# The feed-forward residual over pairs of blocks: output by features, weight leaves stationary, 256 tokens moving

## The chip, the cores and the metric

The kernel runs on one core of a Trainium2 chip. The metric is the device time of one execution in microseconds, the median of three runs. A core has TensorE (PE; its weight loads are listed apart as PEld), VectorE (DVE), ScalarE (ACT), GpSimd (POOL) and SyncE (SP); transfers are issued here from SP and ACT and run on 16 DMA engines. Matmuls write the eight PSUM banks, which GpSimd does not read in this program.

## The reference

A transformer block with conditioning, x of 2 x 2048 tokens by 512 features, all in float32:

```python
emb = jnp.dot(jax.nn.silu(t), ada_w) + ada_b
shift_msa, scale_msa, gate_msa, shift_mlp, scale_mlp, gate_mlp = jnp.split(emb, 6, axis=-1)
norm = _ln(x) * (1.0 + scale_msa[:, None]) + shift_msa[:, None]
h = jax.nn.gelu(jnp.dot(norm, ssm_w1) + ssm_b1, approximate=False)
x = x + gate_msa[:, None] * (jnp.dot(h, ssm_w2) + ssm_b2)
norm2 = _ln(x) * (1.0 + scale_mlp[:, None]) + shift_mlp[:, None]
hf = jax.nn.gelu(jnp.dot(norm2, ff_w1) + ff_b1, approximate=True)
x = x + gate_mlp[:, None] * (jnp.dot(hf, ff_w2) + ff_b2)
```

ff_w1 is 512 x 1024, ff_w2 1024 x 512. Gates, shifts and scales differ between the two batch elements, not between tokens.

## The kernel before

The 4096 tokens are eight blocks of 512 (four tiles of 128). The first part of the program (ssm1, ssm2, norm2) makes x1 = x + gated ssm output for every block and leaves x1 and the normed, turned tokens in DRAM. The second part, the ff part, takes the blocks in four pairs s = 0 to 3: ff1(s) for both blocks at once, then ff2(s, 0) and ff2(s, 1) one block after the other.

All large products use Strassen's scheme in Winograd's form: two halves by two halves give seven products P1 to P7 of half size in place of eight, at the price of sums of the operands (`first` and `second`, four additions each) and of the results. Nested twice, 49 products of quarter size ("leaves") stand for 64.

- ff1 (lines 1025 to 1098): a stage holds seven outer products in the order OUTER, each of seven leaves. The weight leaf is stationary (128 x 128, read from DRAM through a ring of five slots in `ring`), and 256 columns of tokens move: two matmuls a leaf, 98 a stage. Leaves are spread over slots: product n has its leaves at slots 7n, 7n+2, ..., so two products alternate on TensorE. Each leaf is added from its bank into the hidden tile hC by VectorE (or copied by ScalarE), features on partitions, tokens in columns; ScalarE then takes GELU in place.
- ff2 (lines 1115 to 1285): here hidden leaves are stationary and the weights move, 128 columns at a time, so the result comes out by tokens: 49 leaves of two matmuls, 98 a block, 196 a pair (in the first pair P6 is not nested: 8 matmuls of 256 columns replace 14). The results are added from the banks straight onto x1 in the tile rows, and rows is stored, four stores a block. The gate of the ff branch cannot be applied by row, so it is multiplied into ff_w2 beforehand, once per batch element: weight_fw2 for the first, weight_fw2_ahead and weight_fw2_loaded (through DRAM) for the second; the gated bias gb5 is put into the banks before the products begin.

The order on each engine is not written by hand. Every operation is recorded with its reads, writes and costs; `Plan.order` gives each TensorE operation a due time by the sum of the TensorE costs before it, hands these back to all that it depends on, and a list scheduler (`Plan.simulate`) then picks for VectorE, ScalarE, GpSimd and SP the operation that is due first. Additions marked "vg" may go to VectorE or GpSimd; additions that read a bank only to VectorE. Two additions whose operands all lie in SBUF are never placed at the same time on both, by the planner's `lock`. The order so found is the order in the program: an instruction that waits holds all that stand behind it on its engine, transfers on SP and ACT too.

At the end of the program the last block's ff2 stores its quarters as they are finished: the last four VectorE additions each add a leaf's bank onto rows, and stores of 128 KB follow on SP and ACT.

## Time and profile before

| | us |
|---|---|
| median of three runs | 565.51 (565.48 to 566.46) |
| span of the profiled execution, first to last instruction | 563.6 |
| TensorE busy in it | 557.3 |
| VectorE busy | 484.2 |
| GpSimd busy | 377.5 |
| ScalarE busy | 265.3 |
| ff part on TensorE, first matmul to last | 213.46 to 559.97 |

The profiled execution has no time of its own beside its span; the median of the runs stands 1.9 us above that span. In the tables of windows each row is a stretch of the span: its length, then for each engine the busy time and the number of records, then the granted TensorE clock (1.00 is full), the share of the 16 DMA engines' time and what they moved. A float32 matmul is two records, and a busy time of TensorE is not a measure of peak. In a row of groups stand line, engine, operation, output and inputs, shape, count, busy time, mean ns of one, then the engine's idle time before these and what ended it. The line numbers are those of helpers (L294 mm, L304 turn_by_pe, L256 tt, L274 act, L283 copy, L316 dma, L592 turn).

### The profile page before, as it was taken

The numbers are of one execution on the slowest core, as the hardware profiler recorded it, in microseconds if no ns is written. First come the engines' busy times: TensorE is split into PE (matmuls) and PEld (weight loads), VectorE is DVE, ScalarE is ACT, GpSimd is POOL, SyncE is SP. The second block draws the span as 40 slices with busy tenths as digits, with TensorE's granted clock in tenths as the row PEclk, the third lists the DMA queues.
The fourth block names the chain that finished last, engine by engine and source line by source line (L and its number), as shares of the span: only waits on it lengthen the run. The fifth ranks groups of instructions, "written<-read, shape, count | busy, mean of one in ns | idle before, by whom it ended". The sixth has DMA issues, their size and how long they took to land.

```text
span 563.6 us, 10326 instructions
## 1 busy us (share of the span) xinstructions
PE 557.3 (99%) x3553; PEld 506.3 (90%) x3553; DVE 484.2 (86%) x916; ACT 265.3 (47%) x535; POOL 377.5 (67%) x516
## 2 busy tenths in 40 slices
PE   8999999999999999999999999999999999999997
PEld 4888889888898988889998889999889999889997
DVE  5696978888879989898999888989999898789886
ACT  3473866674878845558102346322366222336020
POOL 2887638979826687996656886776785673446670
PEclk9999999999999999999999999999999999999999
DMA  8953799979699788896047989068956041720022
GB/s 315 398 223 84 236 348 317 304 239 323 221 276 368 246 283 267 274 310 203 4 150 246 302 292 318 35 199 283 324 171 203 2 151 44 273 95 30 1 76 74
DMA packets 53057, 119.85 MB, mean 213 GB/s; under 512 B 5473, under 2 KB 10509, under 8 KB 51470
## 3 DMA queue, kind: packets, MB, share of 16 engines
q1 hardware_dynamic: 51842, 118.66, 63.7%
q10 hardware_dynamic: 1164, 0.55, 0.4%
q8 instruction: 28, 0.46, 0.3%
q14 instruction: 23, 0.19, 0.1%
HBM read 77.63 MB, written 40.51 MB: 210 GB/s over the span
## 4 chain that ended last, share of the span: by engine, by line
PE 97%; DMA 1%; DVE 1%; SPq 0%; issue 0%
PE bank L294 96%; DMA fw<-in_L_cond_ada_w_dram 1%; PE bank L304 0%; DVE rows L256 0%; DVE marks L523 0%; SPq L316 0%; DVE ring L256 0%; DVE far L592 0%; DVE turned L657 0%; DVE marks L524 0%; DVE bank L482 0%; DVE mod L485 0%
## 5 line engine op out<-in xcount | busy, mean ns | idle before, releaser
L294 PE MATMUL bank<-turned,ring 128*128 128x256 f32 x896 | 208.6, 380 | 0.2 <-DVE turned L657 0.2
L294 PEld LDWEIGHTS bank<-turned,ring 128*128 128x128 f32 x896 | 167.8, 190 | 22.7 <-DVE turned L657 0.4
L256 DVE TENSOR_TENSOR hidden<-bank,hidden 128x512 f32<-128x512 f32 (+1 forms) x171 | 124.1, 755 | 27.3 <-PE bank L294 25.1
L294 PE MATMUL bank<-near,hidden 128*128 128x256 f32 (+1 forms) x470 | 95.3, 350 | 0.3 <-DVE rows L256 0.2
L294 PEld LDWEIGHTS bank<-near,hidden 128*128 128x128 f32 x470 | 82.1, 190 | 10.0 <-DVE rows L256 0.6
L294 PE MATMUL bank<-fw,hidden 128*128 128x128 f32 x640 | 90.4, 275 | 0.0
L256 DVE TENSOR_TENSOR rows<-bank,rows 128x128 f32<-128x128 f32 (+3 forms) x154 | 79.0, 555 | 10.1 <-PE bank L294 9.3
L294 PE MATMUL bank<-ring 128*128 128x256 f32 x336 | 82.4, 381 | 0.0
L294 PEld LDWEIGHTS bank<-fw,hidden 128*128 128x128 f32 x640 | 81.2, 192 | 0.5
L283 ACT COPY bank<-bank 128x512 f32<-128x512 f32 (+2 forms) x89 | 37.4, 421 | 78.8 <-PE bank L294 77.8
L294 PEld LDWEIGHTS bank<-ring 128*128 128x128 f32 x336 | 63.2, 190 | 10.4 <-ACT bank L283 0.7
L256 POOL TENSOR_TENSOR turned<-turned 128x512 f32<-128x512 f32 (+1 forms) x55 | 61.2, 1125 | 15.1 <-ACT turned L274 9.2
L256 POOL TENSOR_TENSOR hidden<-hidden 128x512 f32<-128x512 f32 (+2 forms) x56 | 49.0, 883 | 29.3 <-DVE hidden L256 11.9
L294 PE MATMUL bank<-fw,far 128*128 128x128 f32 (+2 forms) x644 | 67.6, 278 | 0.5 <-DMA fw<-in_L_cond_ada_w_dram 0.5
L274 ACT ACTIVATE hidden<-hidden,cols 128x512 f32<-128x512 f32 (+1 forms) x66 | 45.3, 713 | 38.4 <-DVE hidden L256 38.2
L294 PEld LDWEIGHTS bank<-fw,far 128*128 128x128 f32 (+1 forms) x644 | 60.9, 167 | 2.5 <-issue 1.5
L294 PE MATMUL bank<-fw,near 128*128 128x128 f32 (+1 forms) x452 | 61.2, 279 | 0.0
L294 PEld LDWEIGHTS bank<-fw,near 128*128 128x128 f32 x452 | 56.0, 192 | 0.4
L256 POOL TENSOR_TENSOR fw<-fw 128x256 f32<-128x256 f32 (+1 forms) x51 | 44.7, 885 | 13.4 <-DVE fw L256 7.2
L274 ACT ACTIVATE turned<-turned,mod,mod 128x512 f32<-128x512 f32 x56 | 41.6, 805 | 9.5 <-DMA turned<-turned 8.5
L256 POOL TENSOR_TENSOR ring<-turned,ring 128x256 f32<-128x256 f32 x37 | 27.3, 747 | 13.6 <-PE bank L294 7.4
L274 ACT ACTIVATE hidden<-bank,cols 128x256 f32<-128x256 f32 x62 | 26.6, 472 | 17.1 <-PE bank L294 16.9
(136 smaller groups left out, 698.7 us busy)
## 6 DMA issues: line engine op xcount, KB each, us to landing
ring<-fw_parts SPq DMA_DIRECT2D x28, 512.0 KB
turned<-far SPq DMA_DIRECT2D x52, 256.0 KB
ring<-fw_parts SPq DMA_DIRECT2D x28, 384.0 KB
rows<-x SPq DMA_DIRECT2D x32, 256.0 KB
turned<-turned SPq DMA_DIRECT2D x32, 256.0 KB
out_dram<-rows SPq DMA_DIRECT2D x28, 256.0 KB
fw_parts<-fw SPq DMA_DIRECT2D x21, 256.0 KB
fw<-in_L_cond_ada_w_dram SPq DMA_DIRECT2D x5, 1024.0 KB
```

The costliest lines, as they stand in the source:

```text
L256: lambda E: E.tensor_tensor(o, a, b, f),
L274: lambda E: E.activation(o, a, func, bias=bias, scale=scale),
L283: plan.add("a", lambda E: E.copy(o, a), [o], [a], {"a": cost}, {"a": cost + 60})
L294: lambda E: E.matmul(o, lhsT, rhs, start=start, stop=stop, skip_group_check=True, **kw),
```

## The change

ff2 is rebuilt in the shape of ff1. It takes a pair of blocks at once (`down`): seven outer products in the order DOWN, each of seven leaves; the leaf of ff_w2 is stationary, 256 columns of the hidden tile move, two matmuls a leaf, 98 a pair. The result comes out by features (features on partitions, tokens in columns) and is summed in `summed`, which has four quarters: blk 0 or 1, lower or upper features. ff1 and ff2 of all pairs form one stream of 56 products (`ff`), each beginning seven slots after the one before; the last product of all starts six slots later still, and so runs alone. ff_w2 is no longer gated: its leaves are made once and kept. ScalarE multiplies the finished quarter by the gate and adds the gated bias, both per partition now. VectorE then turns the quarter back in 32 x 32 squares, four transfers write it to DRAM in bands, one reads it back by tokens, and two additions put x1 (read again, half the features at a time) on it before the store (`quarter_out`). In the last pair three quarters go this way, with stores in halves on SP and ACT; the quarter of the last product is turned back in pieces by TensorE instead (`last_out`), and products P7 and P4 are scaled by the gate as they are added (`scaled_add`).

On TensorE, at the seam of ff1 and ff2 of the first pair, these were the rows (bank numbers; turned and ring are ff1's operands, fw_71 holds the leaves of ff_w2, hidden, near and far the hidden tile and its sums):

```order
L294 MATMUL bank_76<-turned,ring 128x256 x2
L294 MATMUL bank_77<-ring 128x256 x2
L294 MATMUL bank_74<-fw_71,hidden 128x128 x2
L294 MATMUL bank_74<-fw_71,near 128x128 x2
L294 MATMUL bank_73<-fw_71,near 128x128 x4
L294 MATMUL bank_77<-fw_71,hidden 128x128 x2
L294 MATMUL bank_77<-fw_71,near 128x128 x2
```

and these are they now:

```order
L296 MATMUL bank_75<-turned,ring 128x256 x2
L296 MATMUL bank_73<-hidden,fw_71 128x256 x2
L296 MATMUL bank_77<-turned,ring 128x256 x2
L296 MATMUL bank_79<-far,fw_71 128x256 x2
L296 MATMUL bank_76<-turned,ring 128x256 x2
L296 MATMUL bank_73<-far,fw_71 128x256 x2
L296 MATMUL bank_77<-ring 128x256 x2
L296 MATMUL bank_78<-hidden,fw_71 128x256 x2
```

The first ff2 product now alternates with the last of ff1, and each of its instructions moves 256 columns.

On VectorE, the end of the program was this (each row adds a leaf's bank onto rows; two more, of bank_72 and bank_74 as in the middle here, follow):

```order
L256 TENSOR_TENSOR rows<-bank_78,rows 128x2x256
L256 TENSOR_TENSOR rows<-bank_78,rows 128x2x2x256
L256 TENSOR_TENSOR rows<-bank_72,rows 128x2x128
L256 TENSOR_TENSOR rows<-bank_74,rows 128x128
L256 TENSOR_TENSOR rows<-bank_76,rows 128x2x128
L256 TENSOR_TENSOR rows<-bank_76,rows 128x128
```

From the last but one addition of P7 in the last pair on it is now this (rows is `summed`; far in the additions is the x1 tile of the first quarter, in the transposes the tile of the bands; the transposes are those of the quarter r2, blk 1, upper features):

```order
L1049 SCALAR_TENSOR_TENSOR rows<-bank_77,mod_125,rows 128x2x256
L258 TENSOR_TENSOR far<-rows,far 128x512 x2
L1073 STREAM_TRANSPOSE far<-rows 128x4x4x32 x2
L1049 SCALAR_TENSOR_TENSOR rows<-bank_73,mod_125,rows 128x256
L1049 SCALAR_TENSOR_TENSOR rows<-bank_78,mod_125,rows 128x256
L1049 SCALAR_TENSOR_TENSOR rows<-bank_79,mod_125,rows 128x256
```

The additions of the first quarter stand ahead of the last two transposes, and those ahead of all scaled additions of the last product. The last rows of VectorE are these (near takes, in pieces, the quarter that TensorE turned back; the last two rows add x1 to the last two quarters that went through DRAM):

```order
L1049 SCALAR_TENSOR_TENSOR rows<-bank_73,mod_125,rows 128x256
L258 TENSOR_TENSOR near<-bank_72,near 128x2x128
L258 TENSOR_TENSOR near<-bank_74,near 128x2x128
L258 TENSOR_TENSOR near<-rows,near 128x512 x2
L258 TENSOR_TENSOR far<-rows,far 128x512 x2
```

Both quarters that went through DRAM are completed behind all that the last product brings.

On SP, the end was eight stores:

```order
L316 DMA ring<-fw_parts 128x1024
L316 DMA ring<-fw_parts 128x768 x2
L316 DMA out_dram<-rows 128x512 x4
L316 DMA out_dram<-rows 128x2x128 x4
L1501 UNCONDITIONAL_BRANCH
```

and is now this (back_ tensors are the quarters in DRAM, x_7 is x1 of the last block):

```order
L318 DMA back_0_1_116<-far 32x4x256 x2
L318 DMA out_dram<-far 128x2x256
L318 DMA back_1_1_118<-far 32x4x256 x2
L318 DMA rows<-back_0_1_116 128x1024
L318 DMA far<-x_7_87 128x4x256
L318 DMA rows<-back_1_1_118 128x1024
L318 DMA out_dram<-near 128x2x256
L318 DMA out_dram<-near 128x2x128 x2
L318 DMA out_dram<-far 128x2x256
```

The read of quarter back_0_1 stands behind the write of quarter back_1_1, and the read of that one behind a read of x1 into the tile that the first quarter's store has to leave.

The core of the diff:

```diff
@@ -97,6 +98,7 @@
                 due[op.n] = t
                 t += op.cost["p"]
+        due.update((n, t + 6000.0) for n in self.closing)
...
-    def fw2_sixth(plain, leaves):
-        leaves["P6"] = leaves_of(plain, 6)
...
-    def weight_fw2(b, bank):
-        plan.stage = f"weight_fw2 {b}"
...
-        for k in range(KH):
-            tt("v" if bank else "vg", fw2_t[:, k, :], fw2_t[:, k, :], g, ALU.mult)
-        return fw2_operands()
...
-    def weight_fw2_ahead(b):
...
-    def weight_fw2_loaded(b):
...
+    def weight_fw2():
+        plan.stage = "weight_fw2"
+        for k in range(0, KH, 2):
+            dma(fw2_t[:, k : k + 2], fw2[k * P : (k + 2) * P, :].rearrange("(k p) d -> p k d", p=P), lead=100000.0)
+        halves = [(n, slice(n * KH // 2, (n + 1) * KH // 2), slice(n * D // 2, (n + 1) * D // 2)) for n in range(2)]
+        outer = first({f"{e + 1}{o + 1}": fw2_t[:, k, d] for e, _, d in halves for o, k, _ in halves}, thirds(fw2_s), cuts=2)
+        leaves = {}
+        for n, p in enumerate(DOWN):
+            q = {f"{e + 1}{k + 1}": outer[p][:, 2 * k : 2 * k + 2, e * P : (e + 1) * P] for e in range(2) for k in range(2)}
+            leaves[p] = first(q, thirds(fw2_l[:, n]))
+        return leaves
...
+    DOWN = ("P1", "P2", "P3", "P6", "P5", "P7", "P4")
...
+    def chain_banks(n):
+        b = {"y": banks[Y_AT[n % 4]], "x": banks[X_AT[n % 2]], "v": banks[V_AT[n % 2]]}
+        return b
+
+    QUAD = {"P2": "11", "P5": "22", "P6": "12", "P7": "22", "P3": "12", "P4": "21"}
...
+    def scaled_add(o, t, scale):
+        cost = cols(o) / 0.96 + 70
+        plan.add(
+            "v",
+            lambda E: E.scalar_tensor_tensor(o, t, scale, o, ALU.mult, ALU.add),
+            [o],
+            [t, o, scale],
+            {"v": cost},
+            {"v": cost + 85},
+        )
+
+    def columns(s, d, e, blk):
+        k, b = 2 * d + e, (2 * s + blk) // PER_B
+        return gb5[:, k, b : b + 1], mods[5][:, k, b : b + 1]
+
+    def rest_in(s, d, blk, x):
+        half = slice(d * D // 2, (d + 1) * D // 2)
+        dma(x, x1_d[2 * s + blk][:, :, half])
+        return x, out_blk[2 * s + blk][:, :, half]
+
+    def quarter_out(s, d, blk, r, scaled=False):
+        done = summed[:, r]
+        n = quarters[0] % 2
+        for e in range(0 if scaled else 2):
+            act(done[:, e], done[:, e], AF.Identity, *columns(s, d, e, blk))
+        band = cut(bands[n], "p (a c e r) -> p e c a r", a=M, c=C, e=2)
+        for e in range(2):
+            o, a = band[:, e], cut(done[:, e], "p (c a q) -> p c a q", c=C, a=M)
+            plan.add("v", lambda E, o=o, a=a: E.transpose(o, a), [o], [a], {"v": 636}, {"v": 705})
+        closing = s + 1 == NBLK // 2
+        queue = lambda f: "sa"[f % 2] if closing else "s"
+        far_t = back_d[s][d][blk]
+        for f in range(M):
+            dma(far_t[:, f].rearrange("(a q) r -> q a r", a=M), cut(bands[n][f * G : (f + 1) * G], "p (a r) -> p a r", a=M), queue(f))
+        flat = done.rearrange("p e t -> p (e t)")
+        dma(flat, far_t.rearrange("p f r -> p (f r)"))
+        x, to = rest_in(s, d, blk, rest[n])
+        for h in range(2):
+            c = slice(2 * h, 2 * h + 2)
+            o = cut(x[:, c], "p c (e f r) -> p (c e) f r", e=2, f=M)
+            a = cut(flat, "p (f c e r) -> p c e f r", f=M, c=C, e=2)[:, c].rearrange("p c e f r -> p (c e) f r")
+            tt("v" if closing else "vg", o, a, o, ALU.add)
+            if closing:
+                dma(to[:, c], x[:, c], queue(h))
+                plan.closing.append(plan.ops[-1].n)
+        if not closing:
+            dma(to, x)
+        quarters[0] += 1
...
+    def down(s):
+        q = {f"{o + 1}{blk + 1}": hC[:, blk, :, 2 * o : 2 * o + 2, :] for o in range(2) for blk in range(2)}
+        ops = {"P1": q["11"], "P2": q["21"], "P3": q["22"]}
+        inner = {}
+        last = s + 1 == NBLK // 2
+
+        def sums():
+            plan.stage = f"ff2 {s}"
+            a, b, c = whole_s
+            parts("vg", a, q["12"], q["11"], ALU.subtract, 2)
+            parts("vg", b, q["22"], a, ALU.subtract, 2)
+            parts("vg", q["12"], q["22"], q["12"], ALU.subtract, 2)
+            ops.update(P4=c, P5=a, P6=b, P7=q["12"])
+
+        def last_sum():
+            plan.stage = f"ff2 {s}"
+            parts("vg", ops["P4"], q["21"], ops["P6"], ALU.subtract, 2)
+
+        def prepare(n):
+            w = ops[DOWN[n]]
+            v = {f"{k + 1}{h + 1}": w[:, k, :, h * HT : (h + 1) * HT] for k in range(2) for h in range(2)}
+            inner[n] = second(v, thirds(half_s[n % 2]), room=rooms[n % 3] if n < 4 else None)
+
+        def leaf(n, f):
+            p = DOWN[n]
+            bank = chain_banks(14 * s + 7 + n)
+            t = bank[BANK[f]][:, :HT]
+            for k in range(2):
+                mm(t, fw2_leaves[p][f][:, k, :], inner[n][f][:, k, :], f in ("P1", "P5") and k == 0, f in ("P2", "P3", "P4") and k == 1)
+            if f == "P1":
+                copy(bank["x"][:, :HT], t)
+                return
+            quad = QUAD[f]
+            e, h = int(quad[0]) - 1, int(quad[1]) - 1
+            new = f not in ("P7", "P3")
+            part = summed[:, :, e, h * HT : (h + 1) * HT]
+            r0, r1, r2, r3 = [part[:, r] for r in range(4)]
+
+            def add(o, a):
+                tt("v", o, t, a, ALU.add)
+
+            if p in ("P1", "P3"):
+                o = r1 if p == "P1" else r3
+                if new:
+                    copy(o, t)
+                else:
+                    add(o, o)
+            elif p == "P2":
+                add(r0, r1 if new else r0)
+                if f == "P4":
+                    quarter_out(s, 0, 0, 0)
+            elif p == "P6":
+                add(r1, r1)
+            elif p == "P5":
+                add(r2, r1 if new else r2)
+                if f in ("P2", "P7", "P3", "P4"):
+                    tt("vg", r3, r3, r2, ALU.add)
+                    if last:
+                        act(part[:, 1:3], part[:, 1:3], AF.Identity, *columns(s, 1, e, 0))
+                if f == "P4":
+                    quarter_out(s, 0, 1, 3)
+            elif p == "P7":
+                both, wide = part[:, 1:3], t.unsqueeze(1).to_broadcast([P, 2, HT])
+                if last:
+                    scaled_add(both, wide, columns(s, 1, e, 0)[1])
+                else:
+                    tt("v", both, wide, both, ALU.add)
+                if f == "P4":
+                    quarter_out(s, 1, 1, 2, last)
+            elif not last:
+                add(r1, r1)
+                if f == "P4":
+                    quarter_out(s, 1, 0, 1)
+            else:
+                scaled_add(r1, t, columns(s, 1, e, 0)[1])
+                last_out(s, f, quad)
+
+        return sums, last_sum, prepare, leaf
...
+    def last_out(s, f, quad):
+        if not tail:
+            tail["x"], tail["out"] = rest_in(s, 1, 0, cut(kb(near_r, 0, 4), "p (c d) -> p c d", c=C))
+
+        def turned_back(quad):
+            e, h = int(quad[0]) - 1, int(quad[1]) - 1
+            bank = cut(banks[(2, 0)[h]], "p (c e d) -> p c e d", c=2, e=2)
+            for c in range(2):
+                col = slice((2 * h + c) * P, (2 * h + c + 1) * P)
+                turn_by_pe(bank[:, c, e], summed[:, 1, e, col], ident, c == 0 and h not in tail, c == 1)
+            tail[h] = True
+            c, d = slice(2 * h, 2 * h + 2), slice(e * P, (e + 1) * P)
+            x = tail["x"][:, c, d]
+            tt("v", x, bank[:, :, e], x, ALU.add)
+            dma(tail["out"][:, c, d], x, "sa"[e])
+
+        tail.setdefault("due", [])
+        for q in tail["due"]:
+            turned_back(q)
+        tail["due"] = []
+        if f in ("P7", "P2", "P3", "P4"):
+            tail["due"].append(quad)
+        if f == "P4":
+            turned_back(quad)
...
-    def ff2(s, blk, six, wops):
...
+                work.append((f"ff1 {s}", lambda n=n, got=got: got["up"][0](n), lambda f, n=n, got=got: got["up"][1](n, f)))
+            sums, last_sum, prepare, leaf = down(s)
+            at_slot(7 * (first_at + 7) + 7, sums)
+            at_slot(7 * (first_at + 7 + 4) + 3, last_sum)
+            for n in range(7):
+                work.append((f"ff2 {s}", lambda n=n, fn=prepare: fn(n), lambda f, n=n, fn=leaf: fn(n, f)))
+        total = len(work)
+        starts = [7 * n for n in range(total)]
+        starts[-1] += 6
+        for at in range(starts[-1] + 13):
+            for fn in hooks.get(at, ()):
+                fn()
...
-    for s in range(NBLK // 2):
-        if s == 1:
-            fw2_sixth(*ff)
-        if 2 * s == PER_B:
-            ff = weight_fw2_loaded(1)
-            fw2_sixth(*ff)
-        if 2 * s + 2 == PER_B:
-            weight_fw2_ahead(1)
-        ff1(s)
-        if 2 * s + 2 < NBLK and 2 * s + 2 not in SOON:
-            normed2(2 * s + 2)
-        for blk in range(2):
-            ff2(s, blk, *ff)
```

352 lines of the change are left out of this document (74 added, 278 removed).

## Prediction

> **What bounds the kernel now.** I read the page's engine table, then the chain of waits, then a table of windows cut at the stages of the ff part (the ff stages are seen in the timeline of TensorE by their operands: turned and ring for ff1, fw and hidden, near or far for ff2).
>
> ```profile
> PE 557.3 (99%) x3553; PEld 506.3 (90%) x3553; DVE 484.2 (86%) x916; ACT 265.3 (47%) x535; POOL 377.5 (67%) x516
> PE 97%; DMA 1%; DVE 1%; SPq 0%; issue 0%
> 208.18 351.36 PE bank L294 x2348
> 559.56 0.42 DVE rows L256
> 560.01 0.29 DVE rows L256
> ```
>
> TensorE is busy 99% and carries 97% of the chain; from 208.18 to the end it is one piece of 351.36 us that waits for nobody. Only at the end do two VectorE adds follow, and then 563.6 - 560.3 = 3.3 us in which the last stores land. So whatever shortens TensorE's stream shortens the run, as long as the end does not get longer.
>
> ```profile
> core 0: us, PE busy (x) PEld busy (x) DVE busy (x) ACT busy (x) POOL busy (x), PEclk, DMA share, GB/s
> 213.46:255.95 42.49, 42.49 (x197) 37.08 (x196) 38.68 (x63) 23.81 (x39) 39.46 (x53) 1.00 0.92 290
> 255.95:300.62 44.67, 44.67 (x369) 43.73 (x368) 42.15 (x84) 11.75 (x28) 24.07 (x25) 1.00 0.36 119
> 300.62:343.16 42.54, 42.54 (x198) 37.08 (x197) 37.84 (x54) 15.97 (x28) 34.37 (x39) 1.00 0.87 287
> 343.16:387.05 43.89, 43.89 (x394) 43.85 (x393) 39.20 (x79) 15.72 (x39) 30.94 (x33) 1.00 0.57 190
> 387.05:429.73 42.68, 42.68 (x199) 37.08 (x198) 41.63 (x65) 20.12 (x34) 32.59 (x38) 1.00 0.71 233
> 429.73:473.50 43.77, 43.77 (x394) 43.77 (x393) 39.90 (x83) 11.76 (x33) 26.11 (x28) 1.00 0.29 93
> 473.50:515.90 42.40, 42.40 (x198) 36.96 (x197) 34.44 (x51) 17.59 (x30) 21.07 (x24) 1.00 0.44 146
> 515.90:560.00 44.10, 44.07 (x394) 43.85 (x392) 36.95 (x75) 8.97 (x30) 21.29 (x24) 1.00 0.11 35
> ```
>
> The rows alternate ff1, ff2. Both do 49 products of quarter size over a pair of blocks, but ff1 (98 matmuls of 256 columns, about 196 records) takes 42.40 to 42.68 us and ff2 (196 of 128 columns) 43.77 to 44.67. In ff2 the weight loader (PEld) is busy for the whole stage, in ff1 for 37 of 42.5: a load for every 128 columns is not hidden. VectorE is at 36 to 42 of 44 us: little room.
>
> **What TensorE gains.** The new ff2 has the shape of ff1: 49 products, two matmuls of 256 columns each, one new weight leaf per matmul. I price it by the mean of the four ff1 rows, 170.11 / 4 = 42.53. Before, the four ff2 rows sum to 176.43; after, 170.1: **6.3 us less**. Against it stand eight transposes in TensorE at the very end:
>
> ```profile
> 32.04 1.04 PE L304 MATMUL bank<-far 128*128 128x128 f32 x8
> ```
>
> Eight records are four instructions; less about 0.15 of pipeline, 0.22 us each, so 1.8 us for eight. In an unbroken stream TensorE would start the last product at 213.46 + 55 x 42.53/7 = 547.6 and end at 547.6 + 6.1 + 1.8 = 555.5 instead of 560.0: 4.5 us earlier. Row 5 of gates, modulation(5) for gate_rows_of(5), has the same 16 matmuls, so the start of ff I leave at 213.46 (the pre-ff part has about 1 us of idle TensorE to win, and may lose as much).
>
> **What VectorE and GpSimd get.** Prices by form over the ff part:
>
> ```profile
> L256 DVE TENSOR_TENSOR hidden<-bank,hidden 128x512 f32<-128x512 f32 x128 | 85.2, 685 | 16.2 <-PE bank L294 14.3
> L256 DVE TENSOR_TENSOR rows<-bank,rows 128x256 f32<-128x256 f32 x48 | 19.9, 415 | 4.3 <-PE bank L294 3.8 <-issue 0.3
> L256 DVE TENSOR_TENSOR near<-near 128x512 f32<-128x512 f32 x11 | 7.8, 706 | 0.8 <-PE bank L294 0.8
> L592 DVE STREAM_TRANSPOSE far<-near 128x512 f32<-128x512 f32 x3 | 2.1, 699 | 0.0
> L256 POOL TENSOR_TENSOR near<-near,hidden 128x512 f32<-128x512 f32 x9 | 11.5, 1275 | 2.6 <-DVE near L256 2.6
> ```
>
> Per pair the new ff2 gives VectorE 28 adds out of a bank of 256 columns (11.6 us), 6 of 512 (4.1) and 8 transposes (5.6): 21.3 us that only it can do. The rest may go to either engine: 8 sums of 1024 columns, 36 of 512, 4 of 256. In the built order VectorE gets, at these prices, about 81 us of work in the first pair (which still holds the last blocks' norm2 and leaves of fw2) and 72 in the others, of 85; in the old first pair it was 80.8 of 87.2 by the windows. That ran without a stall, so I price the middle at **0.5 us of stalls**, between 0 and the 9.5 of rival (c). The 32 ScalarE gatings (about 0.8 us each) lie in stages where ScalarE is under 60% busy, and the removed gating of ff weights, its second loading and the leaves of the second batch element were all beside TensorE: nothing, both ways.
>
> **What the end gets.** Here I expect the gain to go. A quarter of the output is turned by VectorE, written to DRAM, read back, added to x1, stored. Three quarters of the last pair are so made, and the last of them (blk 1, upper features) is complete only with the last but one product, 6.1 us before TensorE's last matmul. Its queue on VectorE, from the end of the P5 product's last leaf at 547.6 - 4 x 0.87 = 544.1: one add of 0.42, five scaled adds of 512 columns out of banks (3.4; scalar_tensor_tensor on such a tile is not in the trace, and between the 0.42 of a half and the 0.7 of two SBUF operands I take the plain add's 0.685), four transposes (2.8) and two adds of the first quarter (0.7 each, put ahead of the last two transposes): 8.1 us, **552.2**. The same queue holds the scaled adds of the last product, so TensorE waits about 2 us for its y bank there, off the longest path. Then the transfers:
>
> ```profile
> 265.44 0.32 SPq L316 DMA_DIRECT2D near<-gates  x1
> 265.50:266.00 0.50, 0.50 (x7) 0.50 (x6) 0.46 (x3) 0.27 (x1) 0.50 (x1) 1.00 0.00 0
> 266.00:266.50 0.50, 0.50 (x6) 0.50 (x6) 0.50 (x1) 0.00 (x0) 0.50 (x1) 1.00 0.10 33
> 4.00:4.50 0.50, 0.50 (x2) 0.33 (x1) 0.00 (x0) 0.00 (x0) 0.00 (x0) 1.00 1.00 404
> 561.00:561.50 0.50, 0.00 (x0) 0.00 (x0) 0.00 (x0) 0.00 (x0) 0.00 (x0) 1.00 1.00 285
> 561.50:562.00 0.50, 0.00 (x0) 0.00 (x0) 0.00 (x0) 0.00 (x0) 0.00 (x0) 1.00 0.95 283
> 562.00:562.50 0.50, 0.00 (x0) 0.00 (x0) 0.00 (x0) 0.00 (x0) 0.00 (x0) 0.64 0.08 23
> ```
>
> From issue to first bytes 1.0 us (265.44 to about 266.4); loads at full share move 404 GB/s, stores 285, so 512 KB is 1.3 or 1.84 us; the last bytes leave at about 562.1 and the span ends 1.5 later. The bare chain of that quarter: 552.2 + 1.0 + 1.84 written, + 1.0 + 1.3 read, + 0.7 the first half's add, + 0.7 the second's, + 1.0 + 0.92 stored, + 1.5 = 562.2, and 0.3 for two semaphores: **562.5**, the floor. But the transfers are not alone. From 553.2 on seven pieces of 512 KB must move: this quarter's write, read and store, its x1 (its tile is free only when the first quarter's stores are out), the other quarter's read (on SP it stands behind the write) and store, and the stores of the turned-back quarter. Four stores and three loads take 7.4 + 3.9 = 11.3 us: bytes until 564.5, span **566.0**. I take this, since the queue has other bytes in every gap of the chain. With 0.5 of stalls: 566.5, against 563.6 **2.9 us more**. The median of the runs shown is 1.9 above that span, so 568.4; I say **568.0**.
>
> **Rivals.** (a) The likeliest, as above, 0.50; its own range 565.5 to 571. (b) Faster, by the floor: loads run beside stores, so the pieces do not add up, and the chain decides: span 562.5 or a little more, 564.4 in the median. For it: the DMA share in the last ff2 row is 0.11, so nothing older is in the way. Against it: the full share in the rows above. It holds if the pieces overlap by 2.4 us or more. Chance 0.25. The Trainium skill speaks for it: DMA: Bandwidth & Descriptors, Anatomy of one DMA, gives a fixed cost of about 2.0 us to each transfer beside its bytes; by that the chain would end, estimated, near 562.9, and no run here yet shows a chain of this kind.
>
> (c) The port of VectorE and GpSimd. In the old end:
>
> ```profile
> 541.48 1.58 DVE L256 TENSOR_TENSOR far<-far 128x256 f32<-128x256 f32 x1
> 541.50 1.27 POOL L256 TENSOR_TENSOR far<-hidden 128x512 f32<-128x512 f32 x1
> ```
>
> An add of 256 columns, both operands in SBUF, lasts 1.58 us beside a GpSimd add that ends at 542.77: it sat until that was through. So these operations of both engines exclude each other. In the first pair VectorE's are about 27 us and GpSimd's 67, 94.4 where 84.9 are to be had: if nothing can slide into the next pair, TensorE waits 9.5 us in ff2 0, and the time is 577. Against it: the old first pair needs by the same count about 85 of 87 and shows no wait, and GpSimd runs some 5 us ahead into the next pair. Chance 0.15. The Trainium skill states the same as an exclusive lock for the whole instruction (SBUF — State Buffer, two separate sides); the trace agrees by the row above.
>
> (d) The ring of ff1 weights comes late, because on SP the round trips of the last two quarters stand among its loads while the share is already 0.87: perhaps 3 us over three pairs, 571. Against it: the loads are held by their ring slot (TensorE) longer than by the transposes ahead of them. Chance 0.06. (e) ff2 does not get shorter because its bank turnaround stalls it: 44 us a stage, 574. Chance 0.04.
>
> **How the numbers follow.** A difference under 0.2% (1.1 us: 564.4 to 566.6) cannot be told from none. Case b puts 0.17 on faster and 0.08 on no change, case a adds 0.03 and 0.08 to these by errors in its many small terms and 0.39 to slower; c, d and e are slower. Faster 0.20, same 0.16, slower 0.64. The range leaves out the better part of (c) and the best of (b): 563.3 to 573.
>
> **What would show it.** Right: ff2 windows of 42.4 to 42.9 with the loader at 37; TensorE's last matmul near 557 to 558; then 8 or more us with DMA share near 1 and only a few VectorE adds. Wrong: VectorE waits of TensorE in the middle of ff2 (c, e), ring waits in ff1 (d), or a DMA share well under 1 after 553 with an end before 563 (b). The forecast fails if the last quarter's transposes end much before 552 or if loads and stores run side by side.

## The result, and the profile after

| | before | changed kernel |
|---|---|---|
| median, us | 565.76 | 570.7 (569.9 to 571.1) |
| ratio to before, 95% interval | | 1.0087 (1.0073 to 1.0101) |
| span of the profiled execution | 563.6 | 568.1 |
| last matmul of TensorE ends | 559.97 | 557.45 |
| from there to the end of the span | 3.6 | 10.65 |

The changed kernel is 0.9% slower, inside the range (563.3 to 573) and 2.7 us above the 568.0 forecast. TensorE is done 2.5 us earlier than before, and the end that follows it is 7 us longer.

The engine table and the chain of waits of the changed kernel, by engine, from its page:

```profile
PE 553.2 (97%) x2801; PEld 480.6 (85%) x2801; DVE 481.9 (85%) x841; ACT 281.6 (50%) x521; POOL 391.5 (69%) x476
DVE 3%; PE 1%; DMA 1%; issue 0%; DVEq 0%
```

The weight loader has fallen from 506.3 to 480.6 us, as it should with half the loads in ff2. The chain is no longer TensorE from beginning to end: the page follows it back only through the last 33 us, and there it goes by VectorE, by the last product on TensorE (552.64 to 557.47, left out below) and by a transfer. Its end, in order of time (start, length, engine):

```profile
551.42 1.21 DVE far L1073 x2
552.64 0.37 DVE rows L1049
...
557.93 5.46 DMA out_dram<-near
563.38 0.68 DVE far L258
564.07 0.60 DVEq L1436
```

The piece of 5.46 us is put down to a store, but the addition at 563.38 (x1 onto the last quarter, r2) waits for r2's read as well; that read is issued at 557.37. SyncE's queue over the same time shows it (start, length, transfers):

```profile
549.57 0.78 SPq L318 DMA_DIRECT2D back<-far  x2
550.85 0.41 SPq L318 DMA_DIRECT2D out_dram<-far  x1
552.66 1.45 SPq L318 DMA_DIRECT2D back<-far  x2
554.29 0.76 SPq L318 DMA_DIRECT2D rows<-back  x1
555.36 0.82 SPq L318 DMA_DIRECT2D far<-x  x1
557.37 0.34 SPq L318 DMA_DIRECT2D rows<-back  x1
560.88 1.45 SPq L318 DMA_DIRECT2D out_dram<-near  x3
564.10 0.37 SPq L318 DMA_DIRECT2D out_dram<-far  x1
```

r2's bands are written from 552.66, read back from 557.37, added at 563.38, stored from 564.10; the span ends at 568.1. Microsecond by microsecond the transfers moved this (last two columns: share of the DMA engines, GB/s):

```profile
551.00:552.00 1.00, 1.00 (x6) 0.87 (x6) 1.00 (x3) 0.00 (x0) 0.00 (x0) 1.00 0.96 215
552.00:553.00 1.00, 0.71 (x4) 0.28 (x2) 1.00 (x4) 0.00 (x0) 0.00 (x0) 1.00 1.00 264
...
556.00:557.00 1.00, 0.68 (x5) 0.22 (x4) 0.73 (x3) 0.00 (x0) 0.00 (x0) 1.00 1.26 231
...
560.00:561.00 1.00, 0.00 (x0) 0.00 (x0) 0.84 (x2) 0.00 (x0) 0.00 (x0) 0.50 1.10 398
...
564.00:565.00 1.00, 0.00 (x0) 0.00 (x0) 0.67 (x2) 0.00 (x0) 0.00 (x0) 0.50 0.57 184
...
566.00:567.00 1.00, 0.00 (x0) 0.00 (x0) 0.00 (x0) 0.00 (x0) 0.00 (x0) 0.50 0.56 195
```

From 550 to 566.6 all rows together make 4.73 MB, nine pieces of 512 KB, and from 551 to 564 the share lies between 0.71 and 1.26. From 545 to 550 it was 0.

The middle, cut at the first ff1 matmul of each pair, at the first ff2 matmul of the last pair, at TensorE's first wait and at its end (columns as before):

```profile
296.12:381.08 84.96, 84.93 (x393) 74.31 (x392) 74.23 (x116) 37.17 (x64) 62.24 (x56) 1.00 0.61 200
381.08:465.71 84.63, 84.63 (x393) 74.39 (x392) 77.32 (x115) 35.38 (x63) 59.65 (x50) 1.00 0.61 201
465.71:508.64 42.93, 42.85 (x198) 37.08 (x197) 40.44 (x63) 17.73 (x30) 29.31 (x31) 1.00 0.71 230
...
545.06:557.45 12.39, 10.54 (x48) 8.10 (x48) 11.07 (x22) 3.42 (x6) 5.21 (x5) 1.00 0.57 146
```

A whole pair took 86.43 (42.54 + 43.89) before and takes 84.96 and 84.63. In the last 12.39 us TensorE is busy for 10.54; the table of waits (total, times, longest) names what it waited for:

```profile
PE bank L296 <- DVE rows L1049: 1.5, 2, 1.1
PE bank L306 <- DVE rows L1049: 0.3, 1, 0.3
```

Both are the scaled additions of the last two products, at 545.06 (1.08 us), 552.72 (0.43) and before the last transposes (0.32).

### The profile page after: what moved, and what is told of

Read it like the earlier page. It is cut to its first block, busy times and chain, and to the rows that moved or that the text cites. A ratio compares the mean times of both kernels' runs of the same rounds, so it can differ in the third digit from the quotient of the medians.

```text
span 568.1 us, 8720 instructions
## 1 busy us (share of the span) xinstructions
PE 553.2 (97%) x2801; PEld 480.6 (85%) x2801; DVE 481.9 (85%) x841; ACT 281.6 (50%) x521; POOL 391.5 (69%) x476
## 5 line engine op out<-in xcount | busy, mean ns | idle before, releaser
L258 POOL TENSOR_TENSOR turned<-turned 128x512 f32<-128x512 f32 (+1 forms) x65 | 73.6, 1146 | 22.1 <-DVE turned L258 10.2
L296 PE MATMUL bank<-far,fw 128*128 128x256 f32 (+1 forms) x354 | 86.1, 375 | 0.2
L258 DVE TENSOR_TENSOR rows<-bank,rows 128x256 f32<-128x256 f32 (+1 forms) x142 | 65.9, 477 | 15.4 <-PE bank L296 12.6
L296 PEld LDWEIGHTS bank<-far,fw 128*128 128x128 f32 x354 | 66.5, 190 | 10.0 <-issue 0.5
L258 POOL TENSOR_TENSOR hidden<-hidden 128x128 f32<-128x128 f32 (+2 forms) x45 | 45.7, 1025 | 26.7 <-DVE hidden L258 13.2
L296 PE MATMUL bank<-near,fw 128*128 128x256 f32 (+1 forms) x246 | 60.9, 377 | 0.4 <-DVE rows L1049 0.4
L296 PE MATMUL bank<-hidden,fw 128*128 128x256 f32 (+1 forms) x216 | 53.2, 376 | 1.1 <-DVE rows L1049 1.1
L296 PEld LDWEIGHTS bank<-near,fw 128*128 128x128 f32 x246 | 46.3, 190 | 6.9 <-issue 0.8
L296 PEld LDWEIGHTS bank<-hidden,fw 128*128 128x128 f32 x216 | 40.3, 190 | 7.3 <-DVE rows L1049 1.5
L276 ACT ACTIVATE rows<-rows,gb,mod 128x512 f32<-128x512 f32 x32 | 25.5, 812 | 27.0 <-DVE rows L258 18.9
```

Of the source, the lines that this page charges most:

```text
L258: lambda E: E.tensor_tensor(o, a, b, f),
L276: lambda E: E.activation(o, a, func, bias=bias, scale=scale),
L296: lambda E: E.matmul(o, lhsT, rhs, start=start, stop=stop, skip_group_check=True, **kw),
```

## The experiments

The theory T: ff2 in the new form is faster on TensorE, the additions, transposes and transfers beside it cost next to nothing there, and what is lost is lost in the tail, where nine pieces of 512 KB share one rate. Against it stood L (the fixed times of the last quarter's chain), S and P (a loss inside ff2).

| kernel | median, us | ratio to before (95%) |
|---|---|---|
| x_cut | 569.92 | 1.0072 (1.0059 to 1.0084) |
| bytes_cut | 568.57 | 1.0047 (1.0034 to 1.0060) |
| no_trip | 563.37 | 0.9960 (0.9946 to 0.9973) |
| no_mid_out | 572.1 | 1.0114 (1.0099 to 1.0129) |
| short_mid_out | 569.55 | 1.0066 (1.0054 to 1.0079) |
| short_r3_sum | 569.99 | 1.0075 (1.0062 to 1.0089) |
| turn_r2 | 565.92 | 1.0001 (0.9993 to 1.0010) |
| turn_r2_quick | 565.6 | 0.9996 (0.9987 to 1.0004) |
| turn_r2_quick_p5 | 566.57 | 1.0017 (1.0008 to 1.0026) |
| turn_r2_fill | 564.76 | 0.9984 (0.9975 to 0.9993) |
| turn_r2_fill_c | 564.99 | 0.9983 (0.9974 to 0.9993) |

**x_cut and bytes_cut: bytes or fixed times?**

```diff
 def rest_in(s, d, blk, x):
+    if (s, d, blk) == (NBLK // 2 - 1, 1, 1):
+        dma(x[:, :1], x1_d[2 * s + blk][:, :1, half])
+        plan.ops[-1].size *= 4
+        return x, out_blk[2 * s + blk][:, :, half]
```

> The x1 of the very last quarter (r2, blk 1, upper features) is read for one token slice of four only: 384 KB fewer in the tail, the order on the engines otherwise kept (the three other slices of that quarter keep what was in the tile). Theory T (from 551 on the transfers are the bound, and their pieces add up): 384 KB at the 335 to 400 GB/s of the rows behind 559 are 1.0 to 1.2 us, so span 567.0 against 568.1 and 1.1 us less than the changed kernel's median 570.7, 569.6. Rival L (the chain write, read, add, store of that quarter sets the end by its fixed times, and the x1 read lies beside it): no change, 570.7 within 0.3.

Measured: 0.78 less, under T's 1.1 and over L's 0; the intervals of the two ratios overlap, so this alone decides nothing. Nor was the order on the engines kept, though the expectation says so. VectorE in x_cut (the later of the two additions is r0's second):

```profile
550.23 0.73 DVE L258 TENSOR_TENSOR far<-rows,far 128x512 f32<-128x512 f32 x1
...
550.88 1.29 DVE L1077 STREAM_TRANSPOSE far<-rows 128x512 f32<-128x512 f32 x2
...
553.29 0.68 DVE L258 TENSOR_TENSOR far<-rows,far 128x512 f32<-128x512 f32 x1
```

In the changed kernel both additions of r0 stand ahead of r2's last two transposes; here the second stands behind them, and its store on ScalarE's queue goes out behind r2's band writes. So r2's write is issued at 552.20 instead of 552.66, and the 0.78 is not the price of the x1 read alone. bytes_cut has the order of x_cut on every engine, so these two can be compared. It adds:

```diff
-                dma(to[:, c], x[:, c], queue(h))
+                if r == 0:
+                    p, c = ((slice(0, P), slice(0, 1)), (slice(0, 1), c))[h]
+                dma(to[p, c], x[p, c], queue(h))
```

> As x_cut (the last quarter's x1 read for one slice of four), and of the first quarter's two closing stores only a quarter of the first and one partition row of the second are issued: together 384 + 384 KB fewer in the tail, the order kept (the rest of quarter r0 of the last pair is left unwritten). The stores left out belong to another quarter than the one that ends last. Theory T (the transfers share one rate and add up): 384 KB at the 285 GB/s of stores are 1.3 us more than x_cut gained, so 569.9 - 1.3 = 568.6. Rival L (fixed times of the chain of the last quarter): 569.9 as in x_cut, since that chain neither reads nor waits for what is left out but for the x1 tile, which is read early enough.

Measured: 568.57, 1.35 less than x_cut, where T said 1.3 and L nothing; no run of one reaches the range of the other (568.17 to 569.10 against 569.58 to 570.44). r2's read on SyncE, which waits for the landing of r2's write, in x_cut and then in bytes_cut:

```profile
558.33 0.32 SPq L318 DMA_DIRECT2D rows<-back  x1
...
556.35 0.32 SPq L318 DMA_DIRECT2D rows<-back  x1
```

The write is issued at nearly the same time (552.20 and 552.12) and its read can go out 2 us sooner. Stores of a quarter that was long finished delay the quarter that ends last: the transfers of the tail share what moves them. It is not that alone: even here r2's write is issued at 552.12, its read at 556.35 and its addition starts at 561.52.

**no_trip: is it the tail?** The three quarters of the last pair are stored as they stand.

```diff
 def quarter_out(s, d, blk, r, scaled=False):
...
+    if s + 1 == NBLK // 2:
+        to = out_blk[2 * s + blk][:, :, d * D // 2 : (d + 1) * D // 2]
+        for h in range(2):
+            dma(to[:, 2 * h : 2 * h + 2], cut(done.rearrange("p e t -> p (e t)"), "p (c q) -> p c q", c=C)[:, 2 * h : 2 * h + 2], "sa"[h])
+        return
     band = cut(bands[n], "p (a c e r) -> p e c a r", a=M, c=C, e=2)
```

> In the last pair the three quarters r0, r3 and r2 are stored as they are, by features, without being turned, written to DRAM, read back or added to x1 (their values in the output are left so). TensorE's work is the same. Theory T: the tail falls away, the end is TensorE's last transposes (557.4, or up to 1 us earlier since VectorE has 5 to 9 operations fewer in its way), one add, and a store of 128 KB with about 4.5 us to the span's end: span 561 to 562, median 563 to 564.5, so 1 to 2.5 us under the kernel before. Rival S (the new ff2 itself costs what is lost, by stalls of TensorE that the trace does not show as waits): stays at 567 or more in the median.

Measured: 563.37, at the lower end of T; S falls. Without its tail the new ff2 is 2.4 us faster than the kernel before. VectorE has 13 operations fewer here as well, so this run shows where the loss is, not which part of the tail makes it.

**no_mid_out and short_mid_out: does the middle cost nothing?** First the quarters of pairs 0 to 2 were left out altogether:

> In pairs 0 to 2 the finished quarters are not gated, turned, sent through DRAM, added to x1 or stored (the output of these pairs is left unwritten); TensorE's work and the last pair are the same. Theory T (all that is beside TensorE and costs nothing): TensorE's 48 stage products keep their time, the median is 570.7 less 0 to 1.0 (VectorE may come less late into the last product). Rival P (VectorE, GpSimd or the transfers of the quarters slow TensorE in the first three pairs without a wait that the trace names): 3 us or more are gained, 567.5 or less.

It became 1.4 us slower, which neither said. With less to place, the scheduler had chosen other orders, and TensorE waited for leaves of ff_w2 that now stood late (288 to 296: busy 5.67 of 8 us, 7.72 in the changed kernel):

```profile
PE bank L296 <- DVE fw L258: 1.6, 1, 1.6
PE bank L296 <- POOL fw L258: 0.7, 2, 0.5
```

It tells nothing of the quarters. So the same operations were kept in the plan, in their places and at their planned cost, and issued on a few columns:

```diff
     act(done[:, e], done[:, e], AF.Identity, *columns(s, d, e, blk))
+    if s + 1 < NBLK // 2:
+        plan.ops[-1].fn = lambda E: E.activation(few, few, AF.Identity, b, g)
...
     tt("v" if closing else "vg", o, a, o, ALU.add)
+    if not closing:
+        plan.ops[-1].fn = lambda E: E.tensor_tensor(o[:, 0, 0, :8], a[:, 0, 0, :8], o[:, 0, 0, :8], ALU.add)
```

> In pairs 0 to 2 every operation of the finished quarters (gate, transposes, band writes, read, x1, additions, store) is issued at its old place on its engine but on a few columns or rows only (the output of these pairs is left wrong and mostly unwritten); the order on every engine is that of the changed kernel, which no_mid_out did not keep. Theory T (all of it lies beside TensorE): TensorE's periods of 14 products stay at 83.2, 85.0 and 84.6 within 0.3, the median is 570.7 within 0.5. Rival P (VectorE, the port or the transfers of the quarters hold TensorE in steps too small for the table of waits, such as the gaps of 0.2 to 0.4 us near 290): the periods fall by 0.5 us or more each, the median to 569 or less.

The same windows in this kernel:

```profile
296.42:381.03 84.61, 84.61 (x394) 74.48 (x392) 70.50 (x117) 33.49 (x64) 55.76 (x56) 1.00 0.32 103
381.03:465.63 84.60, 84.60 (x393) 74.48 (x392) 67.67 (x116) 32.74 (x62) 53.72 (x50) 1.00 0.31 103
465.63:507.94 42.31, 42.31 (x198) 37.24 (x197) 37.82 (x60) 15.83 (x29) 22.73 (x31) 1.00 0.36 112
```

The periods fall by 0.35, 0.03 and 0.62, 1.0 together, and the median by 1.15. The quarters of three pairs do cost about 1 us, more than T's 0.5 and less than the 1.7 of P: halving the transfers (share 0.61 to 0.31) moved the pair of the second row by 0.03 us. The 0.62 stands in two pauses of TensorE in the changed kernel, which this kernel does not have, and the weight loader names what ended them (the row in the middle is VectorE):

```profile
475.44 1.59 PEld L296 LDWEIGHTS bank<-ring 128*128 128x128 f32 x8 [0.47 <-ACT bank L285]
...
480.71 1.29 DVE L1073 STREAM_TRANSPOSE far<-rows 128x512 f32<-128x512 f32 x2
...
482.63 0.73 PEld L296 LDWEIGHTS bank<-ring 128*128 128x128 f32 x4 [0.41 <-DVE hidden L258]
```

The first ends with a copy by ScalarE that stands behind its gatings of the last quarter of pair 2 (four, 471 to 475), the second with an addition by VectorE that stands behind two transposes of that quarter. This was read; neither was moved alone.

**turn_r2: the quarter that ends last without DRAM.** r2 is turned back by TensorE between the leaves of the last product.

```diff
+    def before_last(s, f):
...
+        for c in range(2):
+            turn_by_pe(bank[:, c, e], summed[:, 2, e, col], ident, c == 0 and h not in nexttail, c == 1)
+        tt("v", x, bank[:, :, e], x, ALU.add)
+        dma(nexttail["out"][:, c, d], x, "sa"[e])
```

> The last but one quarter of the last pair (r2) is turned back by TensorE as r1 is, eight transposes more between the leaves of the last product, its x1 read early into a tile of its own; r0 and r3 still go through DRAM. Nothing is left out. Theory T: 1.5 MB fewer in the tail (write, read and the late x1), TensorE's end 1.8 later less the stalls that VectorE's two transposes and two adds made (about 0.5 to 1): 558.3 to 559.2; then add, store, closing 4.5 to 5: span 563 to 564, median 565 to 566.5, no worse than the kernel before. Rival L2 (the third quarter's round trip, r3, sets the end as soon as r2's is gone): its read is issued near 553.5, its adds end near 558.5 and stores land by 563, the same span, so the end must show which of the two stores was last. Rival S (stalls inside ff2): 569 or more.

Measured: 565.92, 4.8 less than the changed kernel, level with before. As L2 said, r3 became the last: on SyncE its read stands behind stores of r2 that wait for their additions.

```profile
551.56 2.28 SPq L318 DMA_DIRECT2D out_dram<-turned  x2
554.30 0.37 SPq L318 DMA_DIRECT2D rows<-back  x1
```

Its additions start at 559.62, with TensorE's end at 557.92: eight more transposes moved it by 0.5 us, not 1.8. They take 0.9 (below), and the 0.43 of waiting is gone, since VectorE's transposes and two additions are out of the last product's way.

**turn_r2_quick and turn_r2_fill: r3's trip first, then no hole.** r0's additions go to GpSimd, r2's stores to ACT, and r0's stores behind r3's read (quick) or ahead of r3's writes (fill).

```diff
-            tt("v" if closing else "vg", o, a, o, ALU.add)
+            tt(("g" if r == 0 else "v") if closing else "vg", o, a, o, ALU.add)
...
+        if closing and r == 3:
+            for o, a in held:
+                dma(o, a)
         dma(flat, far_t.rearrange("p f r -> p (f r)"))
```

> turn_r2, and the round trip of the third quarter (r3) put first in the tail: the two additions of the first quarter r0 go to GpSimd (off VectorE, 1.4 us), its stores behind r3's read, three of r3's four band writes on SP, r2's stores all on ACT. Bytes are those of turn_r2; nothing is left out. By theory T with what turn_r2 showed (r3's read issued at 554.30 because a store that waited for its addition stood ahead of it, landed at 559.59, its stores last): the read is issued near 552.5 and lands by 556 to 557, r3's stores are out before r1's last store, and the end is r1's: last addition 558.0 to 558.4 and 3.5 us as in no_trip, span 561.5 to 562.5, median 563.3 to 564.5, 1.3 to 2.4 us under the kernel before. Rival B (bytes alone bound the tail, whatever their order): 3.0 MB from 550.5 at 300 GB/s end at 560.5, and 1.5 to close, 562.0 as well; but if the rate is the 250 of the first microseconds throughout, 564 and 566 in the median, no gain.

Measured: 565.6, not to be told from turn_r2. T missed. Rival B's second number (566, no gain) came near, but not its reason: the rate is not 250 throughout, it falls to 72 and is 353 to 370 from 558 to 563. Writes issued at 551.04 had landed only when the read went out, and r0's stores stood behind that read (SyncE, then the windows):

```profile
551.04 1.28 SPq L318 DMA_DIRECT2D back<-far  x3
555.11 0.34 SPq L318 DMA_DIRECT2D rows<-back  x1
...
555.00:556.00 1.00, 1.00 (x7) 0.85 (x7) 0.74 (x2) 0.00 (x0) 0.00 (x0) 1.00 0.48 134
556.00:557.00 1.00, 1.00 (x8) 0.85 (x6) 0.81 (x2) 0.00 (x0) 0.00 (x0) 1.00 0.52 72
```

So this write of 512 KB and its landing took 4.1 us.

> turn_r2_quick with the two stores of the first quarter r0 ahead of r3's band writes and read on SP (GpSimd adds r0 two operations earlier); bytes and TensorE's work are the same, nothing is left out. In turn_r2_quick the transfers moved only 134 and 72 GB/s from 555 to 557, since r3's read (issued 555.11, when its writes of 551.04 had landed) waited and r0's stores stood behind it. Theory V (the end of that kernel is the tail's bytes plus this valley): the 512 KB of r0 move into the valley and before it, the transfers end 1.4 to 1.8 us earlier, median 563.8 to 564.4. Rival G (GpSimd's last sums for the last product come 2.5 us later and TensorE waits for them): 566 to 568. Rival C (the chain of r1: last addition, store, closing) sets the end at last addition + 3.5: 563.6 at the least.

Measured: 564.76, 5.9 under the changed kernel and 0.16% under the kernel before, with an interval clear of 1: of the gain expected about half. SyncE and VectorE at the end:

```profile
548.23 1.61 SPq L318 DMA_DIRECT2D out_dram<-far  x2
549.97 1.53 SPq L318 DMA_DIRECT2D back<-far  x3
554.21 0.34 SPq L318 DMA_DIRECT2D rows<-back  x1
...
558.12 0.42 DVE L258 TENSOR_TENSOR near<-bank,near 128x256 f32<-128x256 f32 x1 [0.20 <-PE bank L306]
558.47 1.28 DVE L258 TENSOR_TENSOR near<-rows,near 128x512 f32<-128x512 f32 x2
```

r3's round trip, 549.97 to 558.47, is no longer waited for; its two additions stand behind r1's last on VectorE, and the end is that order and the closing store (559.75 to 563.0). The hole is not filled, though the stores went ahead of it: from 555 to 556 the transfers moved 75 GB/s here too.

**turn_r2_quick_p5, short_r3_sum, turn_r2_fill_c: TensorE's wait of 1.08 us.** All ask whether r3 += r2 in the last pair makes it.

```diff
-                add(r2, r1 if new else r2)
+                both = part[:, 2:4]
+                tt("v", both, t.unsqueeze(1).to_broadcast([P, 2, HT]), both, ALU.add)
```

> turn_r2_quick, and in the last pair the leaves of product P5 are added to r2 and r3 at once (r2 copied from r1 and r1 added to r3 beforehand), so that r3 += r2, two additions of 1.2 us each beside GpSimd, no longer stand between P5 and the gating of r1 and r2. Theory: TensorE's wait of 1.09 us behind the first scaled addition goes, wholly or half, and the end comes 0.5 to 1.0 earlier than in turn_r2_quick. Rival: VectorE is full there (12 us without a gap), and six leaves of 0.685 in place of 0.415 (1.6 us) plus two additions of 1024 columns that the planner now gives it take the gain back: 0 to 1 us later.

Measured: 566.57, slower by 1.0 than turn_r2_quick, the wait 1.2: as the rival said.

```diff
     tt("vg", r3, r3, r2, ALU.add)
+    if last:
+        plan.ops[-1].fn = lambda E: E.tensor_tensor(r3[:, :8], r3[:, :8], r2[:, :8], ALU.add)
```

> In the last pair the four additions r3 += r2 are issued at their old places on 8 columns of 256 (the lower features of blk 1 of the last pair then lack most of r2); order, transfers and TensorE's work are the same. Theory W: two of these additions, 2.35 us for 512 columns because GpSimd's addition of 1024 columns runs at the same time, hold VectorE's first scaled additions and ScalarE's gating of r1 and r2, and so TensorE's 1.08 us at 545.06. The wait falls to under 0.3, r3's and r2's transposes come 1.0 to 1.5 earlier, and since the transfers start as much earlier, the median falls by 0.8 to 1.2, to 569.5 to 569.9. Rival R: VectorE is late there for its bank additions anyway, the wait stays over 0.7 and the median within 0.4 of 570.7.

Measured: 569.99, 0.7 less, and the wait 0.72, between the two. The row of VectorE says why so little:

```profile
541.45 1.83 DVE L1152 TENSOR_TENSOR rows<-rows 128x8 f32<-128x8 f32 x2
```

Two additions of 8 columns took 1.83 us where 256 columns took 2.35: almost all of it is waiting until GpSimd's addition is through. It falls on the first of the two: 1.75 us here and 2.02 in the changed kernel, the second 0.15 and 0.41. The last experiment moved GpSimd's addition:

```diff
+            if last:
+                c = cut(kb(turned_r, 8, 8), "p (n k c) -> p n k c", n=2, k=2)
...
             parts("vg", ops["P4"], q["21"], ops["P6"], ALU.subtract, 2)
+            for op in plan.ops[-2:] if last else ():
+                op.sooner = 14000.0
```

> turn_r2_fill, and in the last pair the operand of the last product (P4, two additions of 1024 columns) is made in a tile of its own some 14 us earlier, so that GpSimd no longer holds the two additions r3 += r2 (2.35 us for 512 columns from 541.69 on). What short_r3_sum could not take away, the waiting for GpSimd's addition, is taken away here. Theory W: the two additions fall to about 0.85, TensorE's wait of 1.08 us falls under 0.4 and the median by 0.6 to 1.1, to 563.7 to 564.2. Rival M (the waiting only moves: VectorE and GpSimd exclude each other as long 14 us earlier, or another addition of GpSimd takes the place): 564.4 to 566.

Measured: 564.99, as turn_r2_fill; the wait stays. The chain of waits, read backward from TensorE:

```profile
544.07 0.63 DVE rows L258
544.72 0.82 ACT rows L276
545.57 0.76 DVE rows L1049
```

The two additions fell to 0.98, as W said, and the wait was 1.13: behind the addition stands ScalarE's gating of r1 and r2 in place (0.82), and behind that the scaled addition. So W falls as the whole cause. Rival M, whose range holds the time, is there in part: the first row of the chain is the next r3 += r2 (543.98, 0.71 us instead of 0.42), beside another addition of GpSimd (543.13 to 544.41). Three runs show three operations in a row, on two engines, between the P5 product and the bank that P7 needs; what would free it (gating only at the end, as in the other pairs) was not tried.

## Why the prediction was right, and where it was off

| step of the prediction | forecast | measured |
|---|---|---|
| ff2 on TensorE, four stages | 6.3 less | 4.7 less, 5.7 without the stalls in the middle |
| eight transposes in TensorE | 1.8 | 0.9 |
| waits of TensorE in the last products | about 2 | 1.83 |
| TensorE's last matmul | 557 to 558 | 557.45 |
| the last quarter's transposes end | 552.2 | 552.64 |
| stalls in the middle | 0.5 | 1.0 |
| last bytes of the tail | 564.5 | 566.6 |
| closing | 1.5 | 1.5 |
| span | 566.5 | 568.1 |

- **The gain on TensorE** was mis-sized in two terms that cancelled. The transposes, in TensorE's timeline (start, length, count):

```profile
554.09 0.38 PE L306 MATMUL bank<-far,rows 128*128 128x128 f32 x2
554.30 1.03 PE L296 MATMUL bank<-near,fw 128*128 128x256 f32 x4
...
L306 PE MATMUL bank<-far,rows 128*128 128x128 f32 x8 | 1.6, 285 | 0.3 <-DVE rows L1049 0.3
```

  Eight records are the eight transposes: one each, two start within 0.21 us, 0.9 for all. I had taken two records for one, as a float32 matmul leaves. The stream from 212.96 to 557.45 is 344.49 us; less 1.83 of waits and 0.88 of transposes it is 341.8, against 346.51 before: 4.7 where I said 6.3. Of the missing 1.6, 1.0 is what short_mid_out gave back (I had 0.5 for it). The other 0.6 has no full account. In the last 12.39 us, 20 matmuls at the 0.432 of the middle (84.63 / 196), the transposes and the named waits make 11.35; the other 1.04 lies in pauses too short for the table of waits, 0.26 of it at 547.8. No run took these pauses away.
- **The VectorE queue** of the last quarter, 8.1 us from 544.1, ended 0.4 from the forecast, with the two additions of r0 ahead of the last two transposes as read. I had counted five scaled additions of 512 columns; six ran from 544.36 on.
- **The tail**, case (a), was where the gain went, and transfers that delay each other were part of how; no_trip shows the first, bytes_cut against x_cut the second (1.35 us for 0.39 MB). The bytes ended 2.1 us later than forecast, by two terms that give 2.0 of it. At 553.2 I counted seven pieces; but of the 1.05 MB that r3's writes and r0's stores had begun from 549.6 on, 0.37 MB was still to move (by the windows 0.68 MB had gone since 550): 1.2 us at the rate found. And that rate was 303 GB/s (4.05 MB from 553.2 to 566.6), not the 325 of four stores at 285 and three loads at 404: 0.8 us on seven pieces. The 303 is bytes over time; it takes in slower stretches, 221 to 238 from 555 to 559 (r2's read goes out only at 557.37) and 184 from 564 to 565 (r2's additions end at 564.67), so it is not shown to be a limit of the transfers.
- **Rival (b)**, the floor of 562.5, failed on both counts. Loads did not run free beside stores: no row of the tail passes 398 GB/s, where loads alone had moved 404. And the chain itself is longer: I gave a write 2.84 us from issue to landing and a read 2.3; where least moved beside them they took 4.1 (turn_r2_quick) and 4.2 (turn_r2_quick_p5, issued 554.73, addition 558.90). The 0.3 for two semaphores is in no row: from the end of the transposes to the write's issue the trace has 0.02. The Trainium skill's fixed cost of about 2.0 us for a transfer beside its bytes (DMA: Bandwidth & Descriptors, Anatomy of one DMA, which gives it for transfers issued by GpSimd; these are issued from SP and ACT) gives, as an estimate, 3.8 and 3.3: nearer than mine, and still short. With the measured times r2's chain alone is 552.66 + 4.1 + 4.2, 1.3 for both additions and 3.4 from the last store's issue (564.70) to the end: 565.7. So other bytes cost 2.4 us above the chain. In bytes_cut, where the write goes out at 552.12, the same chain ends at 565.1 and the span at 566.4: 1.3 at most is left for fewer bytes without a shorter chain. By this estimate a median near 568 would have come without any delay by other bytes (565.7 + 1.8 = 567.5). That the forecast lies near the result is in part luck: its floor was 3.2 us too low, and the sum of bytes that I took in its place gave a span of 566.0, close to the chain alone by chance.
- **Rival (c)**, the port, made no wait in the middle. In the last pair the mechanism is there: the first r3 += r2 on VectorE takes 2.02 us beside GpSimd where 0.42 is its time alone, and 1.75 when it has 8 columns. The Trainium skill's exclusive lock (SBUF — State Buffer, two separate sides) is what these rows look like; by turn_r2_fill_c, where the pair took 0.98, TensorE's wait does not hang on it alone.
- **Rivals (d) and (e)** fall: no wait of TensorE on a transfer after ff begins, and pairs of 84.6 to 85.0.
- Of the 2.7 us between 568.0 and 570.7, 1.6 are the span. The profiled execution was the fastest of the four (569.9, span + 1.8), the median 0.8 above it, and 0.4 I had rounded off.

## What to carry to other kernels

A change that speeds up the bounding engine is worth what is left when its last result has left the core: list what must still move after the last product and in which order, bytes that other, finished work has under way included. Round trips through DRAM cost little here in the middle, where TensorE's work covers them (twelve quarters, gating and turning included, about 1 us), and one cost 5 us as the last thing in the program; there turning the data on the engine that was made faster was cheaper, even on the bounding engine. To ask what a piece of work costs under a list scheduler, keep its operations in the plan and make them small: leaving them out changes the order of everything else.

## What the runs showed that was not expected

- Removing work made the program slower: 47 of VectorE's 841 operations and all their transfers gone, 1.4 us more, through the order alone (no_mid_out).
- An addition of 8 columns lasted 1.75 us beside a GpSimd addition of 1024 columns, and 0.17 alone (short_r3_sum): the size of an operation does not tell how long it holds its engine.
- The DMA share reads up to 1.26 (556 to 557) and says little of the bytes: at shares near 1 the rows hold 215 GB/s while bands are written in pieces of 1 KB (551 to 552) and 398 while a quarter is read back (560 to 561); in turn_r2_quick a share of 0.52 moved 72.
- The start of the ff part moves by itself between 212.9 and 214.4 from one execution to another, partly by a wait of TensorE for a small early load (1.6 us where it was 214.40, none in others): the span of one execution is not better than that.
